# Reordering VectorE's work in the fifth product of a Strassen-multiplied output projection

## The chip, the cores and the metric

The kernel runs on one core of a Trainium2 chip. A core has a matrix engine (TensorE, "PE" in the profile, with its weight loads as "PEld"), VectorE ("DVE"), ScalarE ("ACT"), GpSimd ("POOL") and SyncE ("SP"). POOL and SP here mainly issue transfers: SP's go through the hardware queue (q1 in the profile), POOL's through the software queue (q0). The metric is device time in microseconds; the median of the runs counts.

## The reference

The inputs are `x` (64 batches of 64 channels by 1024), a table `cw` of 16 matrices of 64 by 64 that each batch indexes by its condition, and a low-rank mixture: A (64 experts x 16 ranks x 1024), B (64 x 1024 x 16) and a router Wr (64 x 1024).

```python
z = einsum('bct,bcd->bdt', x, W[condition])        # conditioning, per batch
scores = zf @ Wr.T                                 # zf: z as 4096 tokens x 1024
top_vals, top_idx = top_k(scores, 16)
G = zeros.at[..., top_idx].set(softmax(top_vals))  # gates, 4096 x 64
h = einsum('nd,krd->nkr', zf, A)                   # 1024 -> 64*16 = 1024
out = x + 2.0 * einsum('nkr,kdr->nd', h * G[:, :, None], B)
```

So there are two large products per token, both 1024 by 1024, in float32: with A (called "h" below) and with B (called "o").

## The kernel before, in words

The 4096 tokens are worked through in eight groups of 512 (`sts[0]` to `sts[7]`). Each of the two large products is done by Strassen's scheme in the Winograd form: seven products `p1` to `p7` of half-size blocks, with sums of blocks ahead of them (operands) and sums of results behind them. From the second group on, and in some products of the first, each of the seven is itself split into seven smaller ones, its leaves. TensorE does the products; VectorE does nearly all sums; ScalarE copies banks of matrix results out of PSUM.

All work is written out as one list, `parents`, in the order in which TensorE takes the products. `run` issues one entry; each entry has hooks at three places, "mid", "late" and "end", to which `at(n, when, f, ...)` ties further work. Every engine works through its own instructions in the order in which they were issued, so the place of a hook sets the order of VectorE's work.

The change is in the first group's "o" product. Its entries begin at index `o` and come in the order

```python
"o": ("p1", "p7", "p2", "p6", "p4", "p5", "p3"),
```

The first five (`p1`, `p7`, `p2`, `p6`, `p4`) are whole products (`whole_parent`, L542): matmuls of 128x512 against a block of B kept in the core. The sixth, `p5`, and the seventh, `p3`, are split a second time (`parent`, L475). The fifth is the entry `o + 4`.

For one of the split products, `prepare` (L500) makes four operands t1 to t4 on VectorE (`l_t` in the profile) from its left operand, and `mm` (L513) uses each of the seven leaves in two matmuls. In `run` the leaves of one product and of the one before it are interleaved. For the sixth and seventh product TensorE takes: the sixth's `p1` and `p2` (straight from its operand `sum_p5`), its `p6` (t2), `p7` (t3) and `p5` (t1); the seventh's `p1` and `p2` (from its operand `sum_p3`); the sixth's `p3` (t4); the seventh's `p6` (its own t2); the sixth's `p4`; the seventh's `p7` and `p5`; then group 1's first product begins.

`run` for the entry `o + 4` issues, in this order: the first half of the fifth product's matmuls; `done` of the entry before it (`p6`), which adds that product's result `m` into two quarters of the output, `into(1, 0, m)` and `into(1, 1, m)`; the "mid" hooks; `prepare` of the next entry, the sixth product; the "late" hooks; the second half of the matmuls; the "end" hooks. The "mid" hooks before the change are `sums(st, "h_sums", "s4")`, which makes `sum_p3` (L90), a load of group 1's x, and `fetches(RING0, "bp0")`, which starts the first five loads of leaf weights. These go through a ring of five buffers: `mm` issues the next load through SP when it has used one (L525, L464).

Leaves of A and B are themselves sums. VectorE makes them in steps (`leaf_steps`, L406 on) in a pool of five staging buffers, `bsum`, and POOL stores each to device memory (L418), from which SP later loads it. Leaves of B appear as `os_p_p`, those of A as `hs_p_p`. `a_steps` holds A's steps; the hook at the end of `o + 3` works off the last two of them, the leaves `p6` and `p4` of A's block `p3`. Since only five staging buffers exist, the last of these needs the buffer of a leaf of B that was made five steps earlier to be free, which is when that leaf's store is complete.

The four quarters of group 0's output stand in tiles `o` (`st["os"][i, j]`), which are loaded with x at first and to which the products are added. Three buffers serve them, so the fourth quarter, `o_01`, is loaded late (`load_res` at the end of `o + 3`, L783, through POOL). Its first use is `into(0, 1, kept["a"])`, in `done` of the fifth product.

## Time and profile before

| what | value |
|---|---|
| median of 3 runs | 785.92 us (785.75 to 786.83) |
| profiled execution, its own time | 787.5 us |
| its span, first to last instruction | 785.7 us |
| mean granted TensorE clock | 0.996 |
| TensorE busy | 772.1 us (98%) |
| VectorE busy | 632.3 us (80%) |
| ScalarE, GpSimd busy | 186.8 us (24%), 74.7 us (10%) |
| traffic to and from device memory | 267 GB/s over the span |

The profile is of one execution, and its own time stands 1.6 us above the median of the runs; it has its own share of work around the span (787.5 less 785.7, 1.8 us). Busy times are sums over the whole span, so a share of 98% says that TensorE stands still in few places, not that it runs at its peak in the others. A line such as L87 or L90 is a helper's (`add`, `sub`), which many steps share; the names of the tiles tell which step it is. Buffer numbers and the numbers in names are left out there, so `sum_p` stands for `sum_p3` and `sum_p5`, `o` for every quarter of the output and `l_t` for t1 to t4. One matmul in the program is a float32 matmul; it stands in the profile as two records, so two matmuls of a leaf are four.

### The profile page before, as it was taken

Reading aid. Unit: us, or ns where it says so; the run is one execution under the profiler, and the core shown is the slowest. Engines: PE = TensorE matmul, PEld = TensorE weight load, DVE = VectorE, ACT = ScalarE, POOL = GpSimd, SP = SyncE. Lnnn points to the kernel's source line nnn. Section 1 sums busy time; section 2 is a strip of 40 time slices with the busy share of each in tenths; the row PEclk is TensorE's granted clock in tenths of the full one; section 3 lists DMA queues with packets and bytes.
Section 4 is the critical chain, followed back from the end, with each engine's and each line's share of the span. In section 5 each row is a group of like instructions: output and inputs, shape, how many; then the busy total and the mean of one; then the engine's idle time right before and its main releaser. Section 6 shows DMA issues by size and latency. Waiting matters only on the chain.

```text
span 785.7 us, 14781 instructions
## 1 busy us (share of the span) xinstructions
PE 772.1 (98%) x5372; PEld 618.6 (79%) x5372; DVE 632.3 (80%) x1327; ACT 186.8 (24%) x496; POOL 74.7 (10%) x103
## 2 busy tenths in 40 slices
PE   9999979999999999999999999999999999999997
PEld 5445458888788888888888888888888888888886
DVE  4888867678788877898788977889768888688977
ACT  1120012223122322223222222222222231222221
POOL 4335523000010020000200001000200000000000
PEclk9999989999999999999999999999999999999999
DMA  9968779755788948887688967889488893687997
GB/s 330 405 220 290 273 251 304 256 186 165 260 252 280 350 126 324 268 299 268 214 291 276 309 225 266 270 279 329 158 308 264 277 354 110 236 255 251 347 373 249
DMA packets 109175, 211.12 MB, mean 269 GB/s; under 512 B 11232, under 2 KB 27616, under 8 KB 108208
## 3 DMA queue, kind: packets, MB, share of 16 engines
q1 hardware_dynamic: 102064, 189.45, 71.1%
q0 software_dynamic: 6608, 19.95, 7.4%
q8 instruction: 43, 0.70, 0.4%
q10 hardware_dynamic: 432, 0.79, 0.3%
q14 instruction: 28, 0.23, 0.1%
HBM read 177.03 MB, written 33.11 MB: 267 GB/s over the span
## 4 chain that ended last, share of the span: by engine, by line
PE 95%; DVE 2%; issue 1%; ACT 0%; POOL 0%; DVEq 0%; POOLq 0%
PE h_p_x L517 23%; PE o_p_x L517 21%; PE h_p_w L517 12%; PE o_p_w L517 11%; PE h_p_y L517 6%; PE o_p_y L517 5%; PE zp L322 4%; PE h_x L558 4%; PE o_w L558 2%; PE h_w L558 2%; PE o_x L558 2%; PE sw L222 1%; DVE o L87 1%; PE gp L302 1%; PE o_y L558 1%
## 5 line engine op out<-in xcount | busy, mean ns | idle before, releaser
L517 PE MATMUL o_p_x<-lo_p_p,l_t 128*128 128x256 f32 x612 | 151.8, 383 | 5.0 <-issue 5.0
L517 PEld LDWEIGHTS o_p_x<-lo_p_p,l_t 128*128 128x128 f32 x612 | 117.3, 192 | 21.9 <-issue 5.4
L87 DVE TENSOR_TENSOR o<-o,m_o_p 128x1024 f32<-128x1024 f32 (+1 forms) x70 | 82.8, 1203 | 0.5
L157 POOL DMA_INDIRECT w_st<-in_cw_dram,idx x32 | 35.6, 1113 | 426.3 <-PE zp L322 410.5
L87 DVE TENSOR_TENSOR m_h_p<-h_p_w,l_a 128x272 f32<-128x272 f32 x49 | 21.6, 440 | 62.5 <-PE h_p_w L517 62.5
L87 DVE TENSOR_TENSOR m_h_p<-m_h_p,m_h_p 128x1088 f32<-128x1088 f32 x49 | 62.3, 1283 | 0.2
L517 PE MATMUL h_p_x<-a,l_t 128*128 128x272 f32 x224 | 60.5, 392 | 0.0
L517 PE MATMUL h_p_w<-lh_p_p,l_t 128*128 128x272 f32 x196 | 53.7, 396 | 1.2 <-issue 1.2
L517 PE MATMUL o_p_w<-lo_p_p,l_t 128*128 128x256 f32 x204 | 54.1, 388 | 0.0
L517 PE MATMUL h_p_x<-lh_p_p,l_t 128*128 128x272 f32 x196 | 52.9, 392 | 0.0
L517 PEld LDWEIGHTS h_p_x<-a,l_t 128*128 128x128 f32 x224 | 42.6, 190 | 8.6
L614 ACT COPY l_b<-h_p_x 128x272 f32<-128x272 f32 x49 | 19.0, 387 | 123.8 <-PE h_p_x L517 116.9
L335 DVE TENSOR_TENSOR hb<-zp,gg 128x512 f32<-128x512 f32 x64 | 40.0, 684 | 9.8 <-PE zp L322 9.8
L517 PE MATMUL h_p_x<-at,l_t 128*128 128x272 f32 x168 | 45.4, 392 | 0.0
L614 ACT COPY l_b<-o_p_x 128x256 f32<-128x256 f32 x51 | 19.0, 373 | 110.2 <-PE o_p_x L517 110.2
L517 PEld LDWEIGHTS h_p_x<-lh_p_p,l_t 128*128 128x128 f32 x196 | 37.2, 190 | 7.5
L517 PEld LDWEIGHTS o_p_w<-lo_p_p,l_t 128*128 128x128 f32 x204 | 38.7, 193 | 5.6
L517 PEld LDWEIGHTS h_p_w<-lh_p_p,l_t 128*128 128x128 f32 x196 | 36.5, 191 | 8.1 <-issue 1.1
L87 DVE TENSOR_TENSOR m_o_p<-o_p_w,l_a 128x256 f32<-128x256 f32 x50 | 21.1, 423 | 24.8 <-PE o_p_w L517 24.8
L322 PEld LDWEIGHTS zp<-w_st,m_h_p 64*64 64x64 f32 x2048 | 31.6, 135 | 8.5 <-issue 8.5
L517 PEld LDWEIGHTS h_p_x<-at,l_t 128*128 128x128 f32 x168 | 31.9, 190 | 6.6
L621 ACT COPY m_h_p<-h_p_x 128x272 f32<-128x272 f32 x49 | 19.0, 387 | 70.6 <-PE h_p_x L517 70.6
(178 smaller groups left out, 1384.4 us busy)
## 6 DMA issues: line engine op xcount, KB each, us to landing
lo_p_p<-o_p_p SPq DMA_DIRECT2D x289, 256.0 KB
lh_p_p<-h_p_p SPq DMA_DIRECT2D x147, 272.0 KB
lo_p_p<-in_b_t_dram SPq DMA_DIRECT2D x64, 256.0 KB
x<-in_x_t_dram SPq DMA_DIRECT2D x31, 512.0 KB
o<-in_x_dram SPq DMA_DIRECT2D x28, 512.0 KB
out_dram<-o SPq DMA_DIRECT2D x27, 512.0 KB
o_p_p<-os_p_p POOLq DMA_DIRECT2D x28, 256.0 KB
b<-in_b_t_dram SPq DMA_DIRECT2D x4, 1024.0 KB
```

Of the source, the lines that this page charges most:

```text
L87: nc.vector.tensor_tensor(o, a, b, ALU.add)
L157: nc.gpsimd.indirect_dma_start(out=w_st[:, i, :], out_offset=None, in_=cw, in_offset=bass.IndirectOffsetOnAxis(ap=idx[:, n : n + 1], axis=0),)
L222: nc.tensor.matmul(sw[r, i, ts(k, K // 2)].rearrange("p (d k) -> p d k", d=2), lhsT=ws[g][r, i, :], rhs=halves(st["z"][i // 2, k])[r, i % ...
L302: nc.tensor.transpose(gp[:, i, :], st["g2"][i].rearrange("p a k -> p (a k)"), ident)
L322: nc.tensor.matmul(zp[b][e * D : (e + 1) * D, c, s, :], lhsT=halves(z)[r, s, c // 2, ds(c % 2 * P + e * D, D)], rhs=ws[g][r, 2 * i + s, :] ...
L335: nc.vector.tensor_tensor(tokens(hb[j, i])[:, :, :, b, :], zp[b], g_ij[:, :, :, b, :], ALU.mult)
L517: nc.tensor.matmul(bank, lhsT=v[:, c, :], rhs=w[:, c, :width], start=first and c == 0, stop=c == 1, skip_group_check=True,)
L558: nc.tensor.matmul(piles[n, s], lhsT=left()[j][:, c, ts(s, P)], rhs=w, start=c == 0 and PILES[kind][j].isupper(), stop=c == CH - 1, skip_g ...
L614: nc.scalar.copy(par["val"][n], par["bank"]["x"])
L621: nc.scalar.copy(before["q"][0][1], before["bank"]["x"])
```

## The change

In the fifth product (`o + 4`) the two sums of `p6`'s result into the output, the making of `sum_p3` and the last two leaves of A are issued behind the sixth product's operands t1 to t4, and not ahead of them. The sums into the output move from `done` into a function of their own, tied to the "late" hook; `sum_p3` moves to the "end" hook; the last two of A's steps move from the end of `o + 3` to the end of `o + 4`, behind `sum_p3`.

VectorE's order becomes: four leaves of B, t1 to t4, two sums into the output, `sum_p3`, two leaves of A, and then as before. On POOL the load of `o_01` now stands ahead of the two stores of A's leaves. TensorE, ScalarE and SP keep their order, and no engine has more or fewer instructions.

```diff
@@ o_whole, done @@
                 elif j == "p6":
                     kept["a"] = m
-                    into(1, 0, m)
-                    into(1, 1, m)
                 elif j == "p4":
...
+        def a_into():
+            into(1, 0, kept["a"])
+            into(1, 1, kept["a"])
+
+        st["a_into"] = a_into
...
     at(o + 3, "mid", sums, st, "h_sums", "s1")
-    at(o + 4, "mid", sums, st, "h_sums", "s4")
+    at(o + 4, "late", lambda: sts[0]["a_into"]())
+    at(o + 4, "end", sums, st, "h_sums", "s4")
...
         (o + 3, b_steps, 4),
-        (o + 3, a_steps, 2),
+        (o + 4, a_steps, 2),
```

## The prediction

> **What bounds the kernel now.** I read the page first, then TensorE's waits, then the chain of waits around the change.

> ```profile
> span 785.7 us, 14781 instructions
> PE 772.1 (98%) x5372; PEld 618.6 (79%) x5372; DVE 632.3 (80%) x1327; ACT 186.8 (24%) x496; POOL 74.7 (10%) x103
> ```

> TensorE (PE) is busy 772.1 of 785.7 us, and 95% of the chain is its own work. Another engine's order matters only where TensorE stands still. Those places are few (line waited for: us in total, times, longest):

> ```profile
> PE o_p_x L517 <- issue: 5.0, 1, 5.0
> PE h_p_w L517 <- issue: 1.2, 1, 1.2
> ```

> The longest is one gap of 5.0 us. The chain (start, us, what) puts it inside the edited product:

> ```profile
> 100.32 0.86 PE o_p_x L517 x4
> 101.19 0.86 PE o_p_y L517 x4
> 102.05 5.04 issue
> 107.08 2.05 PE o_p_x L517 x4
> 109.13 1.71 PE o_p_w L517 x4
> ```

> A group of four matmul records takes 0.86 us before the gap and up to 2.05 us after it. The windows give the reason (us; busy per engine; then PEclk, DMA share, GB/s):

> ```profile
> 102.00:107.00 5.00, 0.05 (x1) 0.00 (x0) 4.91 (x7) 0.00 (x0) 1.26 (x2) 0.94 0.88 297
> 107.10:113.80 6.70, 6.70 (x17) 5.41 (x18) 5.46 (x12) 0.74 (x2) 0.73 (x1) 0.55 0.51 170
> 113.80:120.00 6.20, 6.20 (x30) 5.38 (x30) 3.77 (x10) 1.57 (x5) 1.11 (x2) 1.00 0.83 259
> ```

> The granted clock falls to about half after the gap and recovers near 113.8. In the gap TensorE waits for the sixth product's operands; VectorE (DVE) is busy for 4.91 of those 5.00 us:

> ```profile
> 98.77 0.72 DVE L90 TENSOR_TENSOR hs_p_p<-a 128x544 f32<-128x544 f32 x1
> 102.06 0.73 DVE L90 TENSOR_TENSOR hs_p_p<-a,hs_p_p 128x544 f32<-128x544 f32 x1 [2.57 <-DMA o_p_p<-os_p_p]
> 102.70 2.35 DVE L87 TENSOR_TENSOR o<-o,m_o_p 128x1024 f32<-128x1024 f32 x2
> 104.97 1.22 DVE L90 TENSOR_TENSOR sum_p<-hb,sum_p 128x1024 f32<-128x1024 f32 x1
> 106.11 0.42 DVE L87 TENSOR_TENSOR l_t<-sum_p 128x256 f32<-128x256 f32 x1
> 106.56 0.42 DVE L90 TENSOR_TENSOR l_t<-l_t,sum_p 128x256 f32<-128x256 f32 x1
> ```

> After the sixth product's first two leaves TensorE needs its second `l_t` (t2). It is made from 106.56 to 106.98; the weight load starts at 107.05. "issue" names no releaser, but the 0.07 us is close, and the other candidates are early: the weights' transfer was issued at 85.25, ScalarE's copy of the bank ended at 101.59. In front of t2 stand A's last two leaves (the second waiting 2.57 us for a store to free its buffer), two sums into the output and the seventh operand.

> **The change, part by part.** No instruction is added or removed; VectorE's order moves, and with it POOL's stores.

> *The gap.* Four `l_t` steps take 106.11 to 107.57, 1.46 us. They now start at 98.77, so t2 ends at 98.77 + 0.45 + 0.42 = 99.64. TensorE reaches its use at 102.05: the 5.04 us go.

> *The half clock.* From 107.08 to 113.78 TensorE does four groups in 6.70 us that take 4 x 0.858 = 3.43 at the full rate: 3.27 us go too. Together 8.31 us.

> *What is late next.* Without the gap TensorE runs six groups from 102.05 (three of the sixth product, the seventh's first two, the sixth's fourth) and at 102.05 + 6 x 0.858 = 107.20 wants the seventh product's t2. VectorE by then, in steps from start to start: the `l_t` until 100.23; two sums 2.27 (102.70 to 104.97), 102.50; the seventh operand 1.14, 103.64 (TensorE needs it at 102.05 + 3 x 0.858 = 104.63: covered, and 0.9 us later it would not be); A's two leaves 0.72 + 0.64, 105.00 (their 2.57 us wait is over, as that store has landed by 102.06); the bank sum 0.34, the two `o_w` sums 1.19, 106.53; the sum into `o_01` 1.13, 107.66; t1 0.45, 108.11. From t2's start to the matmul it was 0.52 (106.56 to 107.08): 108.63. ScalarE's copy of the seventh's first bank waits for the bank sum (one `l_r` buffer) and is done near 106.1, ahead of that. So TensorE stands still for 1.43 us. The net is 8.31 - 1.43 = 6.88 us.

> *POOL's queue.* The load of `o_01` (512 KB) moves ahead of A's two stores (272 KB each). It takes the first one's place, issued 99.95; in the trace that one landed at 104.86. At 0.35 MB/us in this stretch (348 GB/s between 100 and 102) its extra 0.245 MB takes 0.7 us: 105.6. VectorE needs it at 106.53. But SP's weight loads now come 6 us sooner: the one issued at 109.16, when TensorE freed its buffer, goes out at 102.95, and the next at 103.8. If from about 104.2 they took half the engines, 0.524 MB at 0.18 MB/us would land at 107.1, and VectorE and then TensorE would wait 0.6 us more. Between 0 and 0.6 I take 0.2, nearer to nothing, as the old order's landing (105.6) is the nearer row. The gain is 6.7 us. The stores of A's leaves now land some 2 us later (106.4 before); their readers come only in the next token group's products, after 128 us. SP's order is the same in both built programs.

> [...]

> *The weight ring.* Five buffers deep here, each load leaves when TensorE frees a buffer. The first load has from 102.95 to 109.49 (108.63 + 0.86). The tightest, group 1's first, leaves at 109.49 and is used after four groups of 0.86 and two of 0.92, at 114.75: 5.26 us. Landings here took 2.4 us (issued 109.16) to 4.0 (issued 118.13): covered; beyond the slot each late us costs one.

> *VectorE behind.* After the `l_t` (109.12) come a bank sum 0.34, two leaves of B 1.42, two bank sums 0.68 and t1 and t2 of group 1's x, 0.87: 112.4, used at 114.75, so its lag is gone. In the trace TensorE used them at 121.50, 6.75 us later. From there TensorE is paced by its own work to the end (650.7 busy of 657 us from 128 to 785), so the shift stays.

> **The time.** The profiled execution took 787.5 us, 1.8 around its span of 785.7, and the runs' median is 785.92. Own time: 787.5 - 6.7 = 780.8, span 779.0. On the median: 785.92 - 6.7 = 779.2.

> **Rivals.** *No second gap* (5%): if VectorE gets through quicker than the steps, the gain is 8.31: 777.6. Against it, every duration is from a row and no wait is left to vanish.

> *The second gap drops the clock too* (7%): 3.3 us more, 782.5. The 5.04 us gap did so; the gap of 1.17 us that ends at 205.34 did not (clock 1.00 from 206 to 210). The new one, 1.4 to 2.0, lies nearer to the latter, but the border is not in the trace.

> [...]

> *Weights late* (6%): POOL's backlog (its queue fills the engines from 97 to 104) meets the earlier loads. At 6.5 us per landing instead of 4.0 the 5.26 us slot loses 1.3 us: 780.5. For it: 0 GB/s between 108 and 110, a rest that is now used. Against: the slots.

> *The stall was not VectorE's* (4%): "issue" names nobody; then nothing moves, 785.9. Against: the 0.07 us.

> *Slower* (2%): the `o_01` load blocks VectorE, all later operands queue behind it. Each us after 106.53 is a us of TensorE's; once the idle time nears 5 us the half clock's 3.3 us return. Landing at 110.1 gives 5.0 + 3.3: as before. At 112 it would be 787.8. Against: it landed by 108.05 with both stores ahead of it.

> **How the numbers follow.** Forecast 76%, own range 778.4 to 780.9: 0 to 0.6 us on the load, the spread of the runs before round their median (-0.2 to +0.9), and 0.4 us for the step sums, an estimate (some twenty starts read to 0.01 us, waits between engines of 0.05 to 0.1 us left out). The range takes in no second gap and late weights, with the same spread: 777.4 to 781.4; outside lie the clock rival, the unchanged and the slower case, 13%. About 0.2% (1.6 us) is what a measurement of this kernel can tell from no change. Faster: 76 + 5 + 7 + 6 = 94%. Same: 4%. Slower: 2%.

> **What would show it.** Right: `l_t` from 98.8 ahead of the output sums; no TensorE gap at 102; a gap of 1.2 to 2.1 us near 107.2 before a matmul that reads `l_t`; PEclk 1.00 throughout 102 to 114; VectorE's 2.57 us wait gone; group 1's products 6.7 us sooner; a span near 779. Wrong: a gap still at 102 (not VectorE), a gap over 3 us with PEclk near 0.5, VectorE waiting for `o<-in_x_dram`, or new gaps ahead of matmuls that read `lo_p_p` or `lh_p_p`.

## The result, and the profile after

| | before | changed |
|---|---|---|
| median of 6 runs each | 786.49 us (785.75 to 786.93) | 782.92 us (780.80 to 783.83) |
| ratio, 95% interval | | 0.9952 (0.9938 to 0.9967) |
| profiled execution, own time and span | 787.5, 785.7 us | 783.22, 781.4 us |
| mean granted clock of the profiled execution | 0.996 | 0.996 |

The kernel became faster, as forecast, but by 3.6 us (786.49 - 782.92; 2.6 to 4.9 by the interval), not by 6.7. The time lies above the top of the range, 781.4.

The page of the changed kernel first.

```profile
span 781.4 us, 14781 instructions
PE 770.3 (99%) x5372; PEld 617.3 (79%) x5372; DVE 631.8 (81%) x1327; ACT 186.2 (24%) x496; POOL 77.3 (10%) x103
```

The instructions are the same in number, and TensorE is busy 1.8 us less (772.1 before): part of the half clock has gone, not all of it. The longest of TensorE's waits (line waited for: total, times, longest, in us):

```profile
PE o_p_x L517 <- issue: 2.4, 1, 2.4
```

The gap of 5.0 us has become one of 2.4. The chain of waits (start, us, what) shows where it is now:

```profile
105.99 0.88 PE o_p_x L517 x4
106.87 0.02 issue
106.89 0.38 ACT m_o_p L621
107.28 1.98 issue
109.25 1.10 PE o_p_x L517 x4
110.36 3.54 PE o_p_w L517 x8
```

No wait stands at 102 any more. The gap opens at 106.85, in front of the seventh product's t2, which is the place that the prediction named. Behind it eight matmul records take 3.54 us; at 0.86 for four they would take 1.73. The windows (us; busy of PE, PEld, DVE, ACT, POOL with counts; PEclk, DMA share, GB/s) say why:

```profile
106.89:110.30 3.41, 1.05 (x5) 0.76 (x5) 3.13 (x7) 0.37 (x1) 0.40 (x1) 1.00 1.05 414
110.30:113.72 3.42, 3.42 (x9) 2.69 (x9) 2.90 (x7) 0.37 (x1) 1.11 (x2) 0.50 0.85 288
113.72:117.10 3.38, 3.38 (x17) 2.88 (x16) 2.34 (x5) 0.76 (x2) 0.05 (x1) 1.00 0.88 263
```

The clock has dropped once more, for 3.41 us. VectorE's timeline (start, us, instruction, in brackets the idle time before it and what ended it) gives the length of the gap:

```profile
98.85 0.42 DVE L90 TENSOR_TENSOR l_t<-l_t,sum_p 128x256 f32<-128x256 f32 x1
...
102.13 1.22 DVE L90 TENSOR_TENSOR sum_p<-hb,sum_p 128x1024 f32<-128x1024 f32 x1
...
105.00 1.27 DVE L87 TENSOR_TENSOR o<-o,o_w 128x512 f32<-128x512 f32 x2
107.13 1.22 DVE L87 TENSOR_TENSOR o<-o,m_o_p 128x1024 f32<-128x1024 f32 x1 [0.86 <-DMA o<-in_x_dram]
108.28 0.42 DVE L87 TENSOR_TENSOR l_t<-sum_p 128x256 f32<-128x256 f32 x1
108.73 0.42 DVE L90 TENSOR_TENSOR l_t<-l_t,sum_p 128x256 f32<-128x256 f32 x1
```

The sixth product's t2 (98.85) now stands ahead of the sums, as the edit says. VectorE is through with the `o_w` sums at 106.27 and then waits 0.86 us for the load of `o_01`, which POOL issued at 99.56 and which landed at 107.11. Everything queued behind that sum, the seventh's t2 with it, is later by as much.

To add up one stretch in all kernels alike, the experiments below give the time from the sixth product's first matmul to group 1's first matmul ("the stretch"): 18.64 us before, 14.81 in the profiled execution of the changed kernel. What follows to the end is 666.92 and 666.85 us. So 3.83 us of the 4.3 between the two spans are made in the stretch; another 0.37 lie ahead of it, as this execution began its sixth product that much earlier.

### The profile page after: what moved, and what is told of

It reads as the page before. It is cut to its first block, busy times and chain, and to the rows that moved or that the text cites. A ratio compares the mean times of both kernels' runs of the same rounds, so it can differ in the third digit from the quotient of the medians.

```text
span 781.4 us, 14781 instructions
## 1 busy us (share of the span) xinstructions
PE 770.3 (99%) x5372; PEld 617.3 (79%) x5372; DVE 631.8 (81%) x1327; ACT 186.2 (24%) x496; POOL 77.3 (10%) x103
## 4 chain that ended last, share of the span: by engine, by line
PE 95%; DVE 2%; DMA 1%; issue 1%; ACT 0%; DVEq 0%; ACTq 0%
PE h_p_x L517 23%; PE o_p_x L517 21%; PE h_p_w L517 12%; PE o_p_w L517 11%; PE h_p_y L517 6%; PE o_p_y L517 5%; PE zp L322 4%; PE h_x L558 3%; PE o_w L558 2%; PE h_w L558 2%; PE o_x L558 2%; DMA x<-in_x_t_dram 1%; PE sw L222 1%; DVE o L87 1%; PE gp L302 1%; PE h_y L558 1%
## 5 line engine op out<-in xcount | busy, mean ns | idle before, releaser
L517 PE MATMUL o_p_x<-lo_p_p,l_t 128*128 128x256 f32 x612 | 150.2, 380 | 2.4 <-issue 2.4
L517 PEld LDWEIGHTS o_p_x<-lo_p_p,l_t 128*128 128x128 f32 x612 | 116.6, 191 | 18.7 <-issue 2.8
L87 DVE TENSOR_TENSOR o<-o,m_o_p 128x1024 f32<-128x1024 f32 (+1 forms) x70 | 82.8, 1202 | 1.4 <-DMA o<-in_x_dram 0.9
L157 POOL DMA_INDIRECT w_st<-in_cw_dram,idx x32 | 38.3, 1196 | 426.4 <-PE zp L322 410.4
L87 DVE TENSOR_TENSOR m_h_p<-h_p_w,l_a 128x272 f32<-128x272 f32 x49 | 21.5, 440 | 62.6 <-PE h_p_w L517 62.6
L87 DVE TENSOR_TENSOR m_h_p<-m_h_p,m_h_p 128x1088 f32<-128x1088 f32 x49 | 62.3, 1283 | 0.2
L517 PE MATMUL h_p_x<-a,l_t 128*128 128x272 f32 x224 | 60.5, 393 | 0.0
L517 PE MATMUL h_p_w<-lh_p_p,l_t 128*128 128x272 f32 x196 | 53.8, 397 | 0.9 <-issue 0.9
L517 PE MATMUL o_p_w<-lo_p_p,l_t 128*128 128x256 f32 x204 | 54.0, 388 | 0.0
L517 PE MATMUL h_p_x<-lh_p_p,l_t 128*128 128x272 f32 x196 | 52.9, 393 | 0.0
L517 PEld LDWEIGHTS h_p_x<-a,l_t 128*128 128x128 f32 x224 | 42.6, 190 | 8.5
L614 ACT COPY l_b<-h_p_x 128x272 f32<-128x272 f32 x49 | 18.9, 385 | 123.7 <-PE h_p_x L517 115.8
L517 PE MATMUL h_p_x<-at,l_t 128*128 128x272 f32 x168 | 45.4, 393 | 0.0
L517 PEld LDWEIGHTS h_p_x<-lh_p_p,l_t 128*128 128x128 f32 x196 | 37.3, 190 | 7.5
L517 PEld LDWEIGHTS o_p_w<-lo_p_p,l_t 128*128 128x128 f32 x204 | 38.7, 193 | 5.6
L517 PEld LDWEIGHTS h_p_w<-lh_p_p,l_t 128*128 128x128 f32 x196 | 36.5, 192 | 7.9 <-issue 1.0
L87 DVE TENSOR_TENSOR m_o_p<-o_p_w,l_a 128x256 f32<-128x256 f32 x50 | 21.1, 422 | 23.2 <-PE o_p_w L517 23.2
L322 PEld LDWEIGHTS zp<-w_st,m_h_p 64*64 64x64 f32 x2048 | 31.6, 135 | 8.6 <-issue 8.6
L517 PEld LDWEIGHTS h_p_x<-at,l_t 128*128 128x128 f32 x168 | 32.0, 190 | 6.5
L621 ACT COPY m_h_p<-h_p_x 128x272 f32<-128x272 f32 x49 | 18.9, 385 | 70.7 <-PE h_p_x L517 70.7
```

The costliest lines, as they stand in the source:

```text
L87: nc.vector.tensor_tensor(o, a, b, ALU.add)
L157: nc.gpsimd.indirect_dma_start(out=w_st[:, i, :], out_offset=None, in_=cw, in_offset=bass.IndirectOffsetOnAxis(ap=idx[:, n : n + 1], axis=0),)
L322: nc.tensor.matmul(zp[b][e * D : (e + 1) * D, c, s, :], lhsT=halves(z)[r, s, c // 2, ds(c % 2 * P + e * D, D)], rhs=ws[g][r, 2 * i + s, :] ...
L517: nc.tensor.matmul(bank, lhsT=v[:, c, :], rhs=w[:, c, :width], start=first and c == 0, stop=c == 1, skip_group_check=True,)
L614: nc.scalar.copy(par["val"][n], par["bank"]["x"])
L621: nc.scalar.copy(before["q"][0][1], before["bank"]["x"])
```

## The experiments

The theory: the changed kernel loses what was forecast of it to two things, the late load of `o_01` (about 0.9 us of the second gap) and a second spell of half clock behind the gap. The rivals: VectorE's own order ahead of t2 makes the gap whatever the load does; the leaves' stores or the weights set the time; the half clock in the kernel before was not worth 3.27 us.

**1. The load of `o_01` through another queue.** ScalarE, and not POOL, issues this load. It also goes out earlier, at 98.39 and not at 99.56, so this experiment tells what the load's lateness costs, not where it comes from.

```diff
-            (nc.sync if g else nc.gpsimd).dma_start(
+            (nc.sync if g else nc.scalar if (i, j) == (0, 1) else nc.gpsimd).dma_start(
```

> The changed kernel with one edit: the load of o_01 is issued by ScalarE, between its copies of the fourth product (94 us) and of the sixth (101 us), not by POOL behind four stores. Theory: VectorE's wait of 0.86 us for that load (to 107.13) goes, t2 of the seventh product is ready 0.86 us sooner, TensorE's gap at its use falls from 2.40 to about 1.5 us, and a gap of that size no longer brings the half clock (3.4 us of it after the 2.40 us gap): span 781.4 - 0.9 - 1.8 = 778.7, PEclk 1.00 from 100 to 120. Rival (the half clock needs less than 1.5 us of idle time): the gap is 1.5 us all the same, but PEclk falls to 0.5 for 3.4 us again and the span is 780.5.

Measured: 780.77 us (779.64 to 783.77), ratio to the kernel before 0.9932 (0.9913 to 0.9951), span 779.1, stretch 12.17. The load is there before VectorE wants it, and VectorE's wait is gone. TensorE's timeline:

```profile
108.41 1.10 PE L517 MATMUL o_p_x<-lo_p_p,l_t 128*128 128x256 f32 x4 [1.45 <-issue]
```

The second gap falls from 2.40 to 1.45 us, which is the prediction's 1.43 without its term for the load. No half clock follows in this execution (1.00 from 106.89 to 113.72). (The slowest of the six runs, 783.77 us, has a mean clock of 0.997, which by the reading in 8 and 10 below means that its clock did drop somewhere.) So the load's wait is 0.95 us of the gap, and the step sum behind 1.43 was right.

**2. The sum into `o_01` behind the seventh product's operands.** The sum leaves `done` of the fifth product and is tied behind the seventh product's `l_t`, which the entry `o + 5` makes.

```diff
                     into(1, 0, pile="w", last=True)
-                    into(0, 1, kept["a"])
...
+        def a_last():
+            into(0, 1, kept["a"])
...
+    at(o + 5, "late", lambda: sts[0]["a_last"]())
```

> The changed kernel with one edit: the sum of the fourth product's result into o_01 goes behind the seventh product's operands. Theory (VectorE's queue alone sets the second gap): t2 no longer stands behind the load nor behind the 1.14 us of that sum; t2 ends near 107.1, TensorE is there at 106.9: gap about 0.3 us, PEclk 1.00, span 781.4 - 2.1 - 1.8 = 777.5, median about 8 us under the kernel before. Rival (the ring of weights is the next bound): TensorE, now 2 us earlier, meets weights that have not landed; gaps of 1 to 2 us ahead of matmuls that read lo_p_p or lh_p_p between 107 and 118, and a span of 778.5 to 779.5.

Measured: 781.10 us (780.12 to 782.03), 0.9929 (0.9914 to 0.9943), span 779.6. TensorE's timeline:

```profile
107.46 1.10 PE L517 MATMUL o_p_x<-lo_p_p,l_t 128*128 128x256 f32 x4 [0.31 <-issue]
109.55 1.13 PE L517 MATMUL o_p_w<-lo_p_p,sum_p 128*128 128x256 f32 x4 [0.99 <-DVE m_o_p L87]
```

The gap at t2 is down to 0.31 us, and a new one of 0.99 stands one group later. It waits for VectorE's next result: the sum `m_o_p<-o_p_w,l_b` (a bank sum: it adds up a bank of PSUM, the memory that TensorE writes its results to), which reads the bank that the sixth product's leaf `p4` overwrites. Neither the theory nor the rival had named this wait; the sum moved out of one place had been put ahead of it.

**3. The refills out of the load's way.** With POOL's load as in the changed kernel, the first three refills of the weight ring are issued by ScalarE, behind its copy of the seventh product's first bank (105.4 to 106.7), and not by SP from 102.6 on.

```diff
-    def fetch(name):
+    held_back = []
+    def fetch(name, queue=nc.sync):
         if to_fetch:
+            if to_fetch[0] in (("o", "p5", "p4"), ("o", "p3", "p7"), ("o", "p3", "p5")):
+                if queue is nc.sync and len(held_back) < 3:
+                    held_back.append(name)
+                    return
...
+            if (par["kind"], par["g"], par["j"]) == ("o", 0, "p3"):
+                for name in held_back:
+                    fetch(name, nc.scalar)
```

> The changed kernel with one edit: the first three refills of the weight ring are issued by ScalarE after its first copy of the seventh product's bank (about 105.6), not by SP as TensorE frees the buffers (102.6, 103.4, 104.3). Theory (these refills share the engines with o_01's load and delay it): o_01 lands by about 105.9 instead of 107.1, VectorE waits 0 to 0.2 us for it, TensorE's second gap is 1.5 to 1.7 us. Rival (its place behind POOL's stores delays it): it lands at 107.1 as before, VectorE waits 0.86 us, the gap stays 2.4 us.

Measured: 783.49 us (782.29 to 784.35), 0.9956 (0.9941 to 0.9971), span 781.7. The load lands at 106.42 instead of 107.11 (105.9 was expected), VectorE does not wait for it, and the gap at t2 is 1.59 us. The load's line in the list of transfers (the last number is us from issue to landing), first in the changed kernel, then here:

```profile
o<-in_x_dram POOLq DMA_DIRECT2D x1, 512.0 KB, 7.5
o<-in_x_dram POOLq DMA_DIRECT2D x1, 512.0 KB, 6.7
```

But now a refill is late, as the second line of TensorE's timeline shows:

```profile
108.57 1.10 PE L523 MATMUL o_p_x<-lo_p_p,l_t 128*128 128x256 f32 x4 [1.59 <-issue]
110.75 2.04 PE L523 MATMUL o_p_w<-lo_p_p,sum_p 128*128 128x256 f32 x4 [1.08 <-DMA lo_p_p<-o_p_p]
```

So the load and the refills do share: with the refills held back to 105.4 it lands 0.7 us sooner (by the other two profiles of the changed kernel, of experiments 8 and 10, the load takes 7.7 and 7.6 us). From 104.2 to 107.1, in the profile of the changed kernel, SP's queue (q1) took 54.0% of the DMA engines' time and POOL's (q0) 37.4%. The two gaps then bring the clock down (0.50 from 110.26 to 113.68), which is taken up below.

**4. All three sums behind the operands.** As in 2, but the two `o_w` sums go along with the sum into `o_01`.

```diff
-                    into(1, 0, pile="w", last=True)
-                    into(0, 1, kept["a"])
...
+        def a_last():
+            into(1, 0, pile="w", last=True)
+            into(0, 1, kept["a"])
...
+    at(o + 5, "late", lambda: sts[0]["a_last"]())
```

> The changed kernel with two sums into o_10 (the fifth product's) and the one into o_01 all behind the seventh product's operands. Theory: t2 of the seventh ends near 105.9, a microsecond before TensorE's use at 106.9; no gap above 0.1 us between 100 and 118, PEclk 1.00, span 777.2, that is 8.3 us less than before and 0.3 us less than with the o_01 sum alone behind. Rival (weights late): as there, gaps ahead of matmuls that read lo_p_p or lh_p_p, span 778.5 to 779.5, and no gain over moving the one sum.

Measured: 781.19 us (780.56 to 782.30), 0.9934 (0.9919 to 0.9948), span 779.0. No gap at t2, but the wait for `m_o_p` grows from 0.99 to 1.54 us (at 109.72), as more now stands ahead of that bank sum. As in 2, what was expected (no gap) did not come, and for the same reason.

**5. The three sums behind the bank sum as well.** As 4, with the hook at "end" in place of "late", and the load of `o_01` through ScalarE as in 1.

```diff
-    at(o + 5, "late", lambda: sts[0]["a_last"]())
+    at(o + 5, "end", lambda: sts[0]["a_last"]())
```

> Both edits that shortened the second gap, taken further: o_01's load on ScalarE's queue, and the three sums of the fourth and fifth product into the output behind the sixth product's bank sum for its fourth leaf, which TensorE waited for (0.99 and 1.54 us) once the seventh's operands were early. Theory (VectorE's order was the whole of it): no gap between 100 and 112, PEclk 1.00, span 777.3, the full 8.3 us. Rival (weights are next): TensorE runs 1.4 us ahead of the kernel with the load alone moved, where a weight load was late by 0.31 us at 117.0; the ring's loads then come late by 1 to 2 us in sum between 107 and 118, ahead of matmuls that read lo_p_p or lh_p_p, and the span is 778.5 to 779.3.

Measured: 779.66 us (779.37 to 780.51, 5 runs) against 786.37, 0.9919 (0.9905 to 0.9933), span 777.6, stretch 10.36. This is the fastest version here. Between 100 and 112 TensorE does not stand still (a window of 12 us):

```profile
100.00:112.00 12.00, 12.00 (x56) 10.43 (x56) 11.86 (x21) 3.00 (x8) 2.93 (x6) 1.00 1.01 309
```

and its waits name what is late next, the leaf weights:

```profile
PE o_p_w L517 <- DMA lo_p_p<-o_p_p: 0.4, 1, 0.4
PE h_p_w L517 <- DMA lh_p_p<-h_p_p: 0.2, 1, 0.2
```

They are late at 114.37 and 115.70, behind the end of the stretch. So with VectorE's order settled the transfers become the bound, the prediction's rival of late weights, at 0.63 us; in the changed kernel itself, which has the second gap ahead of them, no such wait is seen.

**6. A's leaves put back.** The changed kernel with its last edit undone.

```diff
-        (o + 4, a_steps, 2),
+        (o + 3, a_steps, 2),
```

> The changed kernel with one part undone: A's last two leaves stand ahead of the sixth product's operands again, as before the change. Theory: the wait of 2.5 us for the staging buffer is back ahead of the operands; t2 of the sixth ends near 103.2, TensorE waits 1.6 us there, 1 to 1.5 us for the seventh's operand and about 1 us for its t2: three gaps, 3.5 to 4 us in sum; with the clock halved for one or two windows (1.7 to 3.4 us) the span is 781 to 783.5, so most of the change's gain beyond the sums' move comes from the leaves. Rival (the leaves' place costs nothing, VectorE only needs the same work done by 108): span and gaps as with the whole change, 781.4 and one gap of 2.4 us.

Measured: 783.43 us (782.52 to 783.57, 4 runs), 0.9960 (0.9944 to 0.9976), span 781.5, stretch 14.72. The full clock is kept (mean 1.000), but VectorE waits 2.58 us for a staging buffer ahead of the last leaf, and TensorE has three gaps:

```profile
103.42 1.10 PE L517 MATMUL o_p_x<-lo_p_p,l_t 128*128 128x256 f32 x4 [1.64 <-issue]
...
107.45 1.13 PE L517 MATMUL o_p_x<-b,sum_p 128*128 128x256 f32 x4 [1.20 <-DVE sum_p L90]
...
110.95 1.10 PE L517 MATMUL o_p_x<-lo_p_p,l_t 128*128 128x256 f32 x4 [0.65 <-ACT m_o_p L621]
```

3.49 us in sum, against one gap of 2.40. Moving the leaves saves 1.09 us of standing still, and the changed kernel's profiled execution gives this and more back by its half clock: 14.81 against 14.72. (Without it, in experiment 10, the changed kernel's stretch is 13.17.)

**7. TensorE kept busy in the second gap.** Ten identity matmuls, whose results nothing reads, are put into the gap of the changed kernel. They write the PSUM bank that the seventh product's `p7` takes next.

```diff
+        if two and (par["kind"], par["g"], par["j"]) == ("o", 0, "p3"):
+            w = bank("w")
+            for _ in range(10):
+                nc.tensor.matmul(w[:, :P], lhsT=ident, rhs=ident, start=True, stop=True)
...
```

> The changed kernel with ten matmuls of the identity (128x128, results overwritten) put into the second gap, ahead of the wait for the seventh product's t2; VectorE's work is untouched, so the wait ends when it did. Theory (the half clock from 110.30 on is the answer to a stretch of 3.4 us with only 1.05 us of work in it, and costs 1.8 us): the gap shrinks to under 0.5 us, PEclk stays 1.00, the span is 781.4 - 1.8 = 779.6 although TensorE does 2.2 us more. Rival (the half clock comes from something else, or the matmuls delay t2's user): PEclk falls all the same, span 781.4 or up to 0.5 us more.

Measured: 781.84 us (780.73 to 782.08, 5 runs), 0.9938 (0.9924 to 0.9952), span 780.3, stretch 13.27, clock 1.00 throughout. t2 is used no sooner against the start of the stretch, but the matmuls behind it run at the full rate: from t2's use to group 1's first matmul it takes 3.65 us, and 5.34 in the profiled execution of the changed kernel. The second half clock costs 1.69 us. The span was expected at 779.6 and is 780.3. That it was the identity matmuls that kept the clock up is likely but not shown by this profile, since the changed kernel itself keeps it in some executions (next): no run of these five has a mean clock under 0.998, and five of the changed kernel's twelve have.

**8 and 10. The changed kernel again,** first one execution, then five.

> The changed kernel once more, one look, no edit. Theory (the clock is decided stretch by stretch, 3.41 us each, at times that the program does not set; a gap of 2.4 us that falls into two of them leaves both more than half busy): the gap is 2.2 to 2.6 us again, and the half clock may or may not follow; without it the span is near 779.6, with it near 781.4. Rival (a gap of 2.4 us always halves the clock): half clock for 3.4 us, span 781.4.

> The changed kernel once more, timed in five rounds, no edit: the medians so far gave 3.6 us of gain, the two profiled pairs 4.3 and 4.7. Theory (both are the same effect; in some executions the half clock follows the second gap and in others not): a median between 781.8 and 783.0, a ratio within 0.9938 to 0.9967, and single runs some 1.7 us apart according to the clock. Rival (a further loss that only unprofiled executions have): a median above 783.5.

Measured: 782.74 us for the one (span 781.0, stretch 13.28); 783.05 us (781.43 to 784.34) for the five, 0.9959 (0.9946 to 0.9973), the profiled one 781.43 us (span 779.7, stretch 13.17). VectorE's wait for the load is 1.02 and 0.92 us, TensorE's gap 2.56 and 2.45 us. The gap is thus as long as in the first profile, or longer, and yet neither execution shows a half clock, though the same program runs; from t2's use to group 1's first matmul both take 3.65 us, as in experiment 7. The windows of the first (experiment 8) and the second (experiment 10) around the gap:

```profile
104.39:107.80 3.41, 2.69 (x13) 2.03 (x11) 2.38 (x5) 1.12 (x3) 1.83 (x3) 1.00 0.93 296
107.80:111.21 3.41, 1.57 (x7) 1.24 (x8) 3.34 (x8) 0.37 (x1) 0.00 (x0) 1.00 1.06 416
```

```profile
105.16:108.57 3.41, 1.56 (x8) 1.03 (x6) 2.49 (x4) 0.61 (x2) 1.00 (x2) 1.00 0.92 344
```

In the profiles the clock changes only at the borders of such windows of 3.41 us (last section). In these two executions the gap lies across a border, and TensorE is busy 1.57 and 1.56 us in the emptier window. In the first profile it lies in one window and leaves 1.05. By these three profiles, whether the clock drops is thus a matter of where the gap falls, which changes from execution to execution.

The mean clocks of all executions tell how often it drops, but they have to be read with care, for in the profiles the clock is also at half at the very end of the span, when TensorE is done. In that of experiment 1 this end is 2.36 us long and the only half clock, and it alone makes a mean of 0.998. The window (PE, PEld, DVE, ACT, POOL; PEclk, DMA share, GB/s) takes in most of it:

```profile
776.80:779.10 2.30, 0.00 (x0) 0.00 (x0) 0.00 (x0) 0.00 (x0) 0.00 (x0) 0.50 0.40 148
```

A half clock of 3.41 us takes 0.0022 off the mean, and the longest such end in any profile, 2.47 us (experiment 3), 0.0016. So, by these lengths, a mean of 0.997 or less needs a half clock elsewhere too, 0.999 or more rules one of 3.41 us out, and 0.998 leaves it open. It is also why both profiled executions in the first table show 0.996: 6.83 us at half in the middle before, 3.41 in the middle and 2.13 at the end after. Of the twelve executions of the changed kernel five have 0.996 or 0.997 and take 783.4 us in the mean; five have 0.999 or 1.000 and take 781.9; two have 0.998 (783.5 and 783.83 us). The difference of the first two groups, 1.5 us, is close to the 1.69 of experiment 7.

**9. TensorE kept busy in the old gap.** The kernel before, with 18 identity matmuls in its gap of 5.04 us, and nothing moved.

```diff
+        if two and (par["kind"], par["g"], par["j"]) == ("o", 0, "p5"):
+            w = bank("w")
+            for _ in range(18):
+                nc.tensor.matmul(w[:, :P], lhsT=ident, rhs=ident, start=True, stop=True)
...
```

> The kernel before, with 18 matmuls of the identity (128x128, results overwritten) in its gap of 5.04 us, 4.3 us of work at the full rate; VectorE's order is the old one. This tries one term of the sum alone, the half clock after the gap (3.27 us). Theory: the wait itself stays (TensorE gets its operands no sooner), PEclk stays 1.00, and the span falls by 3.2 us, from 785.7 to about 782.5 (ratio 0.996). Rival (the slower groups after the gap are a restart or operands arriving late, not the clock): the groups after the gap still take 1.7 us each for 6 us and the span stays.

Measured: 783.43 us (782.46 to 784.32, 5 runs) against 786.72, 0.9957 (0.9943 to 0.9970), span 781.6, stretch 15.68. TensorE's timeline:

```profile
102.00 4.18 PE L649 MATMUL o_p_w<-ident 128*128 128x128 f32 x36
107.25 1.10 PE L517 MATMUL o_p_x<-lo_p_p,l_t 128*128 128x256 f32 x4 [1.07 <-issue]
```

t2 comes when it came before (107.25; 107.08), but the groups behind it run at the full rate. The stretch is 2.96 us shorter and the median 3.3: the half clock before was worth what the prediction said, 3.27. Here the idle matmuls did keep the clock: the kernel before shows the half clock in both its profiles (experiment 11 is the second), and the five runs here have mean clocks of 0.999 and 1.000. Work that does nothing is worth about as much as the whole change (0.9957 and 0.9952).

**11. The kernel before, profiled again.**

> The kernel before, unchanged, profiled a second time. In the first execution (own time 787.5 us) the stretch from the sixth product's first matmul to group 1's first took 18.64 us, with a gap of 5.04. The sums made from it come out about 1 us above the gains that the medians show (5.6 against 4.6 for executions of the changed kernel at full clock, 4.0 against 3.0 for those with the half clock). Theory: the stretch itself is always the same, and the first execution was slow by 1 us elsewhere, so that the gain in the stretch is real and about 1 us is lost again elsewhere in the changed kernel: then the stretch takes 18.4 to 18.9 here as well, at a time near 786.5. Rival: the stretch of the first execution was long by some 1 us (its gap or its half clock): then it takes 17.4 to 18.0 here at a time near 786.5, and the medians agree with the sums.

Measured: 787.2 us, span 785.4; a gap of 5.06 us, a stretch of 18.56, and 666.5 us behind it. The stretch is the same as in the first profile (18.64), which speaks for the theory; but the time is not near 786.5, so this execution doesn't show where the medians lose the rest.

## Why the prediction was right, and where it failed

**The first gap (5.04 us) was VectorE's order: right.** With t2 ahead of the sums it is gone, at no cost in front of it: `sum_p3` was in time, as worked out (done at 103.35, used at 104.10).

**The half clock before (3.27 us): right.** Experiment 9 takes it away alone and gets 2.96 us in the stretch, 3.3 in the medians.

**The second gap: right in place and mechanism.** The execution after began its sixth product 0.37 us earlier than before's. Counted with that, TensorE should have stood still from 106.83; it did from 106.85. With the load's wait taken away the gap is 1.45 (experiment 1); 1.43 was worked out.

**"Between 0 and 0.6 I take 0.2": the first step that failed.** VectorE waited 0.86, 0.92 and 1.02 us. The upper bound had the landing right, 107.1 (that the weight loads would take half the engines was its assumption; measured were 54.0%, experiment 3), and measured were 107.11 and (experiment 10) 107.03; but the choice went to "nearer to nothing, as the old order's landing (105.6) is the nearer row". That 105.6 was worked out from a store that had landed at a time without refills in the way, and the change itself put three into it. This is only part of the error: from issue to landing 5.65 us were reckoned, the load took 7.5, and with the refills held back (experiment 3) still 6.7. What makes the other 1.1 us was not tried. Even 0.6 was short, for VectorE was ready at 106.27 and not at 106.53, and the load was not earlier with it.

**"*The second gap drops the clock too* (7%)": the second.** It happened in the profiled execution, and by the mean clocks in five to seven of twelve. The step that failed is its measure: "The new one, 1.4 to 2.0, lies nearer to the latter" compares lengths of gaps. In the profiles the clock goes by windows of 3.41 us (last section), and the gap of 2.40 us left 1.05 us of work in one of them. Its price was too high as well: 1.69 us, not 3.3, since here one window at half rate follows and before there were two. The drop is not all of the miss: the five executions without it take 781.9 us in the mean, which is still above the range.

**What the sum left out.** A first group after a gap takes 1.10 us from its start to its end, where in an unbroken row each group ends 0.86 us after the one before it: 0.24 us. With the measured terms, 8.31 - 2.40 - 0.24 - 1.69 = 3.98 us, against 18.64 - 14.81 = 3.83 in the stretch; without half clock, in experiment 10, 8.31 - 2.45 - 0.24 = 5.62 against 18.64 - 13.17 = 5.47. The steps so corrected close to 0.2 us.

**No second gap, weights late, slower, nothing changed: rightly small.** In the changed kernel no matmul of the stretch waits for weights. But the margin was thinner than worked out: the four weight loads issued from 102.6 to 106.9 took 4.9 to 5.4 us to land, where the prediction reckoned with 2.4 to 4.0, and without the second gap (experiment 5) two later ones are late.

**What stays open.** In the medians the gain is smaller than in the stretch: 786.5 - 781.9 = 4.6 us for executions at full clock, 3.1 for the five that clearly had the half clock, so 0.7 to 0.9 us less. The other kernels that have the new order lose as much (experiment 1: 6.47 in the stretch, 5.8 in the medians; experiment 5: 8.28 and 6.7, of which 0.63 are the late weights), and experiment 9, with the old order, does not (2.96 and 3.3). Both profiled executions of the kernel before took longer than its median (787.5 and 787.2), with the stretch the same. Waits elsewhere change from execution to execution (near 735 us, `zp` L322, 1.1 us in the first profile of after, 0.7 in experiment 11, none in experiment 9), though the instructions there are the same; what sets them wasn't tried. The prediction was also laid on a median of three runs, 785.92, which is some 0.6 us below the later ones; with 786.5 the same gain would have given 779.8.

## What to carry to other kernels

When operands are moved ahead of sums, follow the queue down to the next result that another engine needs, and the one after it: the wait went from the sixth's t2 to the seventh's t2, then to a bank sum, then to the weights, and only at the end of that chain (experiment 5, 779.66 us) was nearly all of the gain there (8.28 of 8.31 us in the stretch). A transfer that a change brings nearer to its use is to be costed with all transfers that the same change brings forward; here the first three refills cost the load of `o_01` 0.7 us (experiment 3). And a gap of TensorE had two prices here: its length (5.04 us before the change), and the half clock behind it (3.27 us), which matmuls that do nothing saved in experiment 9 (2.96 us of the stretch).

## What the runs showed of the clock

```profile
106.85:110.26 3.41, 1.23 (x5) 0.68 (x4) 3.34 (x8) 0.74 (x2) 0.56 (x1) 1.00 0.95 251
110.26:113.68 3.42, 2.93 (x7) 2.42 (x8) 1.69 (x5) 0.00 (x0) 1.11 (x2) 0.50 1.02 394
```

So here the border lies between 1.85 and 2.18 us of idle time in one window. With a border of 2.0 (between the two), a gap of 2.45 us empties a window far enough in (3.41 - 2.45 + 2 x 0.45) / 3.41 = 55% of positions, an estimate, beside the five to seven of twelve. The way back is stricter than the way down, by the few cases here: the window above, with 0.49 us idle, was followed by the full clock; the one in the kernel before was not:

```profile
106.35:109.76 3.41, 2.67 (x6) 2.19 (x7) 3.38 (x8) 0.37 (x1) 0.28 (x1) 0.50 0.29 114
109.76:113.18 3.42, 3.42 (x9) 2.70 (x8) 2.18 (x6) 0.37 (x1) 0.45 (x1) 0.50 0.83 266
```

It had 0.73 us idle, the end of the old gap (0.94 in experiment 11), and a second window at half rate followed. That second window is the difference between 3.27 and 1.69 us.
